# Layer 0's fixed order: where the mean square, the turned-back outputs and the scores for maxima stand

## The chip, the cores and the metric

The kernel runs on one core of one Trainium2 chip. The metric is the device time of one execution in microseconds, the median of the runs shown. A core has five engines that run side by side, each strictly in the order of its own instruction list: TensorE (PE, with its weight loads as PEld), VectorE (DVE), ScalarE (ACT), GpSimd (POOL) and SyncE (SP, which only issues DMAs here). An engine that waits for an operand holds up all that stands behind it in its list.

## The reference

Eight sequences of 256 rows of 512 numbers go through two layers. Each layer adds a gated cross-attention to x and then a gated feed-forward.

```
x = x + tanh(g_xattn[0]) * L0_xattn(layernorm(x), ctx, ctx)   # 16 heads of 32, causal, no weights
x = x + tanh(g_ffn[0])   * L0_ffn(layernorm(x), ...)          # ternary weights, silu(gate)*up,
                                                              # rms_norm over 2048, projection
x = x + tanh(g_xattn[1]) * L1_xattn(layernorm(x), ctx, ...)   # q, k, v, o weights, rms_norm of q and k
x = x + tanh(g_ffn[1])   * L1_ffn(layernorm(x), ...)          # 8-bit activations, ternary weights
```

Layer 0's attention is softmax(q k^T / sqrt(32)) v, with the rows above the diagonal masked; q is the normed x, and k and v are both the context. Its feed-forward is

```
gu = x @ ternary(w_gate_up)^T ; h = silu(gate) * up
out = (h / sqrt(mean(h*h) + eps)) @ ternary(w_proj)^T
```

The mean square is a number for each row, so the kernel multiplies by it behind the projection.

## The kernel before

The 2048 rows are 16 tiles of 128 rows, two for each of the 8 batches. The program has three parts. The first quantizes layer 0's weights, prepares layer 1's keys and values and runs layer 0's attention for batches 0 and 1. The second runs layer 0's feed-forward for batch b (class Feed0), beside layer 0's attention for batch b + 2 (class Attention0), and measures and quantizes layer 1's weights (L922 to L966). The third runs layer 1. The change edits the second part; the attention's `done` of batches 0 and 1 is also used in the first part and at its end.

**How the order is set.** `at(b, (k, step), ...)` gives each step a place: batch b, chunk k, in sixteenths of a batch. `timeline` sorts all steps by place and calls them. In the second part `pe.held` is true, and every PE instruction is tied behind the one called before it, so PE's list is the list of places. The lists of DVE, ACT, POOL and SP are made by a scheduler that follows its own model of the times; the called order is only its priority.

**The feed-forward.** A batch has 16 chunks (8 for each tile of rows). In chunk n PE makes 32 gate/up products into one of two banks "gu" (`hidden`). ACT takes a tanh, DVE multiplies twice (h, L842 and L843; the second one frees the bank), ACT casts the high half (hs, L845), DVE or POOL makes the low half (L295), ACT squares (L848) and POOL adds the square to a sum (acc, L850). Three chunks later PE makes the down product of that chunk into the one bank "y" (`project`). After eight chunks POOL folds the sum (L853), PE adds it over the partitions (`factor`: ssq, into the one bank "o"), DVE and POOL make the power -1/2 of it (rs_t L268, rs_r L270, rgf L887), and DVE adds y, scaled, to x (`add`, L892). `factor` stands before the down product number 7 - AHEAD0 of eight, so with AHEAD0 = 1 before the last but one.

**The attention.** The 16 heads are four groups of four. There are two large score slots (`pair`, PSUM), used in turn by all of the following.

- `ready`: load, layernorm (DVE statistics L277, POOL power L270, POOL y L290), and the turn of y into qT ("turned", PE, then an ACT copy).
- `looks`: four `scores`, each into both slots, DVE takes their maxima (nm, L407, four operations; L415, two, in layer 1's form), then `parts`, ten small POOL operations that split the maxima into three (mz, L427 to L434), then `shift`, where PE turns them (nt) and DVE copies them (nT, L445).
- `weighs`: for each group `exps` (scores the other way round minus the maxima, into both slots, then exp on ACT, p, L481) and `weigh` (products with v and sums into bank "o", copied by ACT, L505, sums added by POOL, L508).
- `done`: PE turns the outputs back ("back", in a score slot) and the sums ("sums", in bank "o"), DVE takes the reciprocal (inv, L569), multiplies (L575) and adds to x (L581).

Behind `done` of batch b + 1 follows Feed0's `ready` of that batch: a layernorm of x, a split into high and low halves (yp, ACT L815 and DVE L816) and a DMA on SP that turns it (xT<-yp).

In the second part the attention of the last batches is followed by `ready` and `looks` of layer 1's attention for batches 0 and 1; its query products ("lin", two halves) take a score slot too, in batches 5 and 6.

The places of the steps before, for the attention that is looked at in batch n:

```
jobs += at(n, *zip((-4.8, -2.4, 4.2 if n == 0 else 0.2), a.ready()))
jobs += at(n, *zip((*((5.4, 7.2) if n == 0 else (1.2, 5.2)), 9.2, 10.4, 10.8, 14.6), a.looks()))
jobs += at(n, *zip((15.3, 18.2, 19.2, 20.2, 22.2, 23.2, 24.2, 25.2), a.weighs()))
jobs += at(n, (27.7, *a.done()))
```

A place over 16 lies in the batch after: 27.7 is chunk 11.7 of batch n + 1.

Of the kernel before, what the change touches and what calls it, by code (L numbers as in the profile page):

```python
# [39 lines left out]
F32 = mybir.dt.float32  # L40
# [5 lines left out]
ALU = mybir.AluOpType  # L46
# [4 lines left out]
P = 128  # L51
B, S, D = 8, 256, 512
NT = B * S // P
NH, HD = 16, 32
DC = D // P
# [22 lines left out]
MP = 3  # L78

LAG = 3  # L80

AHEAD0 = 1

YB = 4

# [4 lines left out]
def flamingo_kernel(  # L90
# [24 lines left out]
    nc = tc.nc  # L115
# [4 lines left out]
    small = ctx.enter_context(tc.tile_pool(name="small", bufs=4))  # L120
    att = ctx.enter_context(tc.tile_pool(name="att", bufs=2))
# [4 lines left out]
    def bank(tag, shape=(P, 512), dtype=F32, name=None):  # L126
        pool, n = part_ps[tag]
        return pool.tile(list(shape), dtype, tag=tag, name=name or tag, bufs=n)

    def banks(stack, name, **tags):  # L130
        pool = stack.enter_context(
            tc.tile_pool(name=name, bufs=1, space=PSUM, reuse_waits="tile")
        )
        part_ps.clear()
        part_ps.update({tag: (pool, n) for tag, n in tags.items()})

    def pair(shape, dtype=F32, name="s"):

        return ps.tile(list(shape), dtype, tag="s", name=name, bufs=2)

    xs = {}
    stage = {}

    def reach(i, n):
        assert stage.get(i, 0) == n - 1, (i, n)
        stage[i] = n
# [4 lines left out]
    def load_x(i, pool):  # L151
        xs[i] = pool.tile([P, D], F32, tag=f"x{i}", name=f"x{i}", bufs=1)
        nc.sync.dma_start(out=xs[i], in_=xf[i * P : (i + 1) * P, :])
# [4 lines left out]
    tg = const.tile([P, 4], F32, name="tg")  # L158
# [4 lines left out]
    ident = const.tile([P, P], F32, name="ident")  # L163
# [97 lines left out]
    pe = Tensor()  # L261
# [96 lines left out]
    class Attention:  # L358
# [3 lines left out]
        n = 0  # L362
# [171 lines left out]
    class Attention0(Attention):  # L534
# [19 lines left out]
            return self.counted(0, [load, norm, turn])  # L554

        def done(self):
            def add():

                t = pair((P, 2, D), name="back")
                sums = bank("o", (P, 2, P), name="sums")  # L560
                for i in range(2):
                    rows = slice(i * P, (i + 1) * P)
                    for c in range(DC):
                        pe.transpose(
                            t[:, i, c * P : (c + 1) * P], self.oT[:, c, rows], ident
                        )
                    pe.transpose(sums[:, i, :], self.sums[:, rows], ident)
                inv = small.tile([P, 2, DC, 4], F32, tag="inv", name="inv", bufs=2)
                nc.vector.reciprocal(  # L569
                    inv, sums.rearrange("p i (r g e) -> p i g r e", r=4, g=DC)[:, :, :, :, 0]  # L570
                )
                for i in range(2):
                    xt = xs[2 * self.b + i]
                    w = self.oT[:, 2 * i : 2 * i + 2, :].rearrange("p c t -> p (c t)")
                    nc.vector.tensor_tensor(  # L575
                        w.rearrange("p (h c) -> p h c", h=NH),
                        t[:, i, :].rearrange("p (h c) -> p h c", h=NH),
                        inv[:, i].rearrange("p g r -> p (g r)").unsqueeze(2).broadcast_to([P, NH, HD]),
                        ALU.mult,
                    )  # L580
                    nc.vector.scalar_tensor_tensor(  # L581
                        xt, w, tg[:, 0:1], xt, ALU.mult, ALU.add
                    )
                    reach(2 * self.b + i, 1)

            return self.finish([add])

    def load_w(pool, name, wT):
        w = pool.tile([P, DC, D], F32, tag=f"w{name}", name=f"w{name}", bufs=1)
# [8 lines left out]
    def timeline(*jobs):  # L598

        steps = []  # L600
        for j, (a, z, job) in enumerate(jobs):
            steps += [(a + (z - a) * (n + 0.5) / len(job), j, step) for n, step in enumerate(job)]
        for _, _, step in sorted(steps, key=lambda e: e[:2]):
            step()

    def at(b, *steps):

        return [(b + n / 16, b + n / 16, [step]) for n, step in steps]
# [150 lines left out]
    att0 = [Attention0(b) for b in range(B)]  # L759
    with ExitStack() as part:  # L760
# [16 lines left out]
        a, z = att0[0], att0[1]  # L777
# [18 lines left out]
    class Feed0:  # L796
# [72 lines left out]
        def step(self, n):  # L869

            if n < HC:
                self.hs[n] = self.hidden(n // 8, n % 8)
            n -= LAG
            if n >= 0:
                if n % 8 == 7 - AHEAD0:
                    self.factor(n // 8)
                self.project(n % 8, self.hs.pop(n))
                if n % 8 == 7:
                    self.add(n // 8)
# [10 lines left out]
        def add(self, i):  # L890
            xt = xs[2 * self.b + i]
            nc.vector.scalar_tensor_tensor(xt, self.ys, self.rg, xt, ALU.mult, ALU.add)  # L892
            reach(2 * self.b + i, 2)
# [35 lines left out]
    def measure1(u):  # L929
        seen[0] += 1  # L930
        w = load1(u)
        a = q1.tile([P, QW], BF, tag="q", name="a1", bufs=2)
        behind(nc.scalar.activation(a, w, AF.Abs, accum_out=l1sum[:, u : u + 1]), block["A"])
# [17 lines left out]
    def quantize1(u):  # L951

        seen[1] += 1
        assert seen[0] == n1
        w = load1(u)
        _, dst, k = units1[u]
        ins = nc.gpsimd.tensor_scalar(w, w, wscale[:, k : k + 1], MAGIC, ALU.mult, ALU.add)  # L957
        behind(ins, block["P"])
        hold1()
        q = q1.tile([P, QW], BF, tag="q", name="q1", bufs=2)  # L960
        nc.gpsimd.tensor_scalar(q, w, 1.0, -MAGIC, ALU.mult, ALU.add)  # L961

        def hold():
            q8 = q1.tile([P, QW], F8, tag="q8", name="q8", bufs=2)
            nc.vector.tensor_scalar(q8, q, 1.0, -1.0, ALU.min, ALU.max, saturate=False)
            nc.sync.dma_start(out=dst, in_=q8.bitcast(U8))  # L966

        left.append(hold)
# [73 lines left out]
    with ExitStack() as part:  # L1042
        banks(part, "ps1", o=1, gu=2, y=1)
        q1 = part.enter_context(tc.tile_pool(name="q1", bufs=1, side="right", reuse_waits="tile"))
        feed0 = [Feed0(b) for b in range(B)]

        def rows(b):
            load_x(2 * b, x2)
            load_x(2 * b + 1, x2)

        jobs = [
            (0.5, 3.0, [lambda u=u: measure1(u) for u in range(n1)]),
            (3.05, 3.05, [scales1]),
            (3.1, 6.5, [lambda u=u: quantize1(u) for u in range(n1)]),
            (6.6, 6.6, [hold1]),
        ]

        jobs += at(0, *zip((-5.0, -4.0), feed0[0].ready()), (-4.5, *att0[1].done()))
        for b in range(B):
            jobs += at(b, *((k, step) for k, step in enumerate(feed0[b].chunks())))
            if b == 0:
                jobs += at(b, *zip((4.4, 5.4), feed0[1].ready()))
            elif b + 1 < B:
                jobs += at(b, *zip((12.4, 13.4), feed0[b + 1].ready()))
        for n, a in enumerate([*att0[2:], *att1[:2]]):
            if n < B - 2:
                jobs += at(n, (-11.0, lambda n=n: rows(n + 2)))  # L1070
                jobs += at(n, *zip((-4.8, -2.4, 4.2 if n == 0 else 0.2), a.ready()))
            else:
                jobs += at(n, *zip((-9.6, -7.6, -4.8, -3.7, -2.6, -2.5, 0.2), a.ready()))
            jobs += at(n, *zip((*((5.4, 7.2) if n == 0 else (1.2, 5.2)), 9.2, 10.4, 10.8, 14.6), a.looks()))
            if a is not att1[1]:
                jobs += at(n, *zip((15.3, 18.2, 19.2, 20.2, 22.2, 23.2, 24.2, 25.2), a.weighs()))
            if n < B - 2:
                jobs += at(n, (27.7, *a.done()))
        pe.held = True
        timeline(*jobs)  # L1080
    w0ctx.close()
# [196 lines left out]
    jobs = []  # L1278
    for b in range(B):
        first, second, a = feed1[2 * b], feed1[2 * b + 1], att1[b]  # L1280
# [76 lines left out]
```

## Time and profile before

| what | value |
|---|---|
| median of 3 runs | 1248.93 us (1246.83 to 1250.46) |
| the profiled execution's own time | 1244.33 us |
| its span, first to last instruction | 1242.6 us |
| mean granted TensorE clock | 0.97 |
| PE, DVE, ACT, POOL busy | 1113.8, 823.0, 611.2, 550.0 us |
| second part (232.5 to 776.0) | 543.5 us |

The profile is one execution. "Granted clock" is the share of full speed that TensorE was allowed. In a row of the timeline the first two numbers are the start and the length in us, then engine, line, operation, output<-inputs, sizes and count; the square brackets give idle time of the engine before it and what ended that. Rows of equal neighbours are merged. In a row of waits the numbers are the total in us, how often, and the longest.

### The profile page before, as it was taken

The numbers are of one execution on the slowest core, as the hardware profiler recorded it, in microseconds if no ns is written. First come the engines' busy times: TensorE is split into PE (matmuls) and PEld (weight loads), VectorE is DVE, ScalarE is ACT, GpSimd is POOL, SyncE is SP. The second block draws the span as 40 slices with busy tenths as digits, with TensorE's granted clock in tenths as the row PEclk, the third lists the DMA queues.
The fourth block names the chain that finished last, engine by engine and source line by source line (L and its number), as shares of the span: only waits on it lengthen the run. The fifth ranks groups of instructions, "written<-read, shape, count | busy, mean of one in ns | idle before, by whom it ended". The sixth has DMA issues, their size and how long they took to land.

```text
span 1242.6 us, 29878 instructions
## 1 busy us (share of the span) xinstructions
PE 1113.8 (90%) x12466; PEld 725.7 (58%) x12565; DVE 823.0 (66%) x1776; ACT 611.2 (49%) x1108; POOL 550.0 (44%) x821
## 2 busy tenths in 40 slices
PE   7988977799999897888999998899999999999976
PEld 3444433577777666666666775455555555555553
DVE  5677797764656455375654645777777777768684
ACT  3446547356575533433344453356464645464663
POOL 3333224353343556465564424826263535424250
PEclk9998888899999998999999999999999999999998
DMA  8343424622333233223222002311212121211231
GB/s 320 127 137 114 158 85 119 221 61 96 120 99 118 64 99 82 82 70 95 84 76 66 19 18 71 109 52 31 64 35 60 35 61 35 61 35 31 39 51 43
DMA packets 101767, 103.91 MB, mean 84 GB/s; under 512 B 61312, under 2 KB 72576, under 8 KB 101632
## 3 DMA queue, kind: packets, MB, share of 16 engines
q1 hardware_dynamic: 98608, 97.01, 26.6%
q10 hardware_dynamic: 3024, 4.98, 1.3%
q8 instruction: 98, 1.61, 0.5%
q14 instruction: 37, 0.30, 0.1%
HBM read 72.09 MB, written 15.73 MB: 71 GB/s over the span
## 4 chain that ended last, share of the span: by engine, by line
PE 29%; DVE 27%; POOL 12%; ACT 8%; issue 5%; DMA 1%; POOLq 0%; DVEq 0%; ACTq 0%
PE gu L256 10%; PE o L256 5%; PE s L256 5%; DVE nm L415 4%; PE y L256 3%; PE py L256 2%; DVE u L1193 2%; DVE h L843 2%; POOL acc L850 2%; DVE ln_st L277 2%; POOL w L957 2%; DVE t L1191 2%; DVE h L842 2%; POOL q L961 2%; DVE umax L1194 2%
## 5 line engine op out<-in xcount | busy, mean ns | idle before, releaser
L256 PE MATMUL gu<-xT,gu 128*128 128x128 f16 x4096 | 254.9, 221 | 11.7 <-DVE h L843 8.3
L256 PEld LDWEIGHTS <-gu 128*128 128x128 bf16 x4096 | 237.7, 99 | 42.2 <-issue 18.6
L850 POOL TENSOR_TENSOR acc<-acc,h 128x256 f32<-128x256 f32 x112 | 83.5, 745 | 130.6 <-ACT h L848 127.0
L256 PE MATMUL gu<-gv,zT 128*128 128x256 fp8e4 x1024 | 131.4, 274 | 10.9 <-ACT gv L1186 6.4
L1186 ACT COPY gv<-gu 128x512 f32<-128x512 f32 x128 | 74.0, 585 | 116.2 <-PE gu L256 108.3
L256 PEld LDWEIGHTS <-zT 128*128 128x128 bf16 x1024 | 96.0, 98 | 57.4 <-issue 36.7
L845 ACT CAST hs<-h 128x256 f16<-128x256 f32 x128 | 51.7, 404 | 147.0 <-DVE h L843 146.6
L842 DVE SCALAR_TENSOR_TENSOR h<-h,gu 128x256 f32<-128x256 f32 x128 | 53.3, 416 | 102.3 <-ACT h L841 97.0
L256 PE MATMUL y<-pr,hs 128*128 128x512 bf16 x413 | 113.5, 383 | 6.9 <-issue 1.4
L270 POOL TENSOR_TENSOR rs_r<-rs_t,mhalf 128x1 f32<-128x1 f32 (+1 forms) x88 | 60.7, 694 | 129.0 <-DVE rs_t L268 108.1
L481 ACT ACTIVATE p<-s 128x768 f32<-128x768 f32 (+1 forms) x128 | 109.8, 908 | 15.1 <-PE s L256 15.1
L415 DVE TENSOR_REDUCE nm<-s 128x4 f32<-128x1024 f32 x64 | 75.8, 1217 | 33.9 <-PE s L256 33.9
L848 ACT ACTIVATE h<-h,hid 128x256 f32<-128x256 f32 x112 | 56.6, 507 | 70.1 <-POOL hs L295 46.6
L508 POOL TENSOR_TENSOR oT<-oT 128x256 f32<-128x256 f32 x48 | 35.3, 735 | 124.3 <-ACT oT L505 124.1
L256 PE MATMUL s<-qT,kT 32*128 32x256 f32 (+1 forms) x1024 | 78.2, 377 | 2.5 <-DVE rs_t L268 1.1
L295 POOL TENSOR_TENSOR hs<-h,hs 128x256 f16<-128x256 f32 x64 | 44.5, 695 | 77.8 <-ACT hs L845 77.8
L841 ACT ACTIVATE h<-gu 128x256 f32<-128x256 f32 x128 | 48.5, 379 | 56.9 <-PE gu L256 56.7
L1191 DVE SCALAR_TENSOR_TENSOR t<-t,gv 128x512 f32<-128x512 f32 x64 | 46.4, 725 | 41.6 <-ACT t L1190 41.6
L256 PE MATMUL s<-kT,qT 32*128 32x256 f32 (+1 forms) x1024 | 68.9, 378 | 2.0 <-DVE nm L415 1.3
L407 DVE TENSOR_REDUCE nm<-s 128x2 f32<-128x256 f32 (+1 forms) x128 | 62.9, 551 | 11.6 <-PE s L256 11.3
L256 PE MATMUL o<-p,v 128*32 128x256 f32 (+1 forms) x1024 | 64.2, 370 | 5.8 <-DVE x L1223 5.6
L256 PEld LDWEIGHTS <-hs 128*128 128x128 f16 x512 | 45.6, 101 | 35.4 <-issue 4.7
(185 smaller groups left out, 2195.4 us busy)
## 6 DMA issues: line engine op xcount, KB each, us to landing
w<-in_gvT_dram SPq DMA_DIRECT2D x32, 512.0 KB, 3.8
w<-in_guT_dram SPq DMA_DIRECT2D x32, 256.0 KB, 3.0
w<-in_outT_dram SPq DMA_DIRECT2D x16, 512.0 KB, 3.6
cT<-in_cxT_dram SPq DMA_DIRECT2D x8, 512.0 KB, 4.9
x<-in_x_dram SPq DMA_DIRECT2D x16, 256.0 KB, 6.6
kT<-in_cxT_dram SPq DMA_DIRECT2D x8, 512.0 KB, 4.0
v<-in_cx_dram SPq DMA_DIRECT2D x8, 512.0 KB, 3.8
vd<-v SPq DMA_DIRECT2D x8, 512.0 KB, 5.3
```

The costliest lines, as they stand in the source:

```text
L256: return self.kept(nc.tensor.matmul(*args, **kwargs))
L270: nc.gpsimd.tensor_tensor(r[:, :n], t[:, :n], mhalf[:, :n], ALU.pow)
L407: nc.vector.tensor_reduce(nm[:, :, qb], s[j][:, :, at[qb] : at[qb] + to[qb]], AX.X, ALU.max, negate=True,)
L415: nc.vector.tensor_reduce(nm, s[j].rearrange("p r (q k) -> p r q k", q=2), AX.X, ALU.max, negate=True)
L481: exp[0] = nc.scalar.activation(self.p[j], s[j][:, :, 0:n], AF.Exp)
L841: block["A"] = nc.scalar.activation(h, gu[:, 0], AF.Tanh, scale=0.5 / UP0)
L842: nc.vector.scalar_tensor_tensor(h, h, 1.0, gu[:, 0], ALU.add, ALU.mult)
L845: nc.scalar.copy(hs[:, 0], h)
L848: nc.scalar.activation(sq, h, AF.Square, scale=hid[:, 1:2])
L850: block["P"] = nc.gpsimd.tensor_tensor(self.acc[i], self.acc[i], sq, ALU.add)
L1186: nc.scalar.copy(self.gv[:, :, k % 2, :], gu)
L1191: nc.vector.scalar_tensor_tensor(t, t, 1.0, g, ALU.add, ALU.mult)
```

## The change

Four things move in the second part, and one tile changes.

1. `factor` stands before the last of the eight down products (n % 8 == 7), one chunk later. AHEAD0 is gone.
2. `done` is two steps, one for each tile of rows, at chunk 26.6 and 27.6 instead of one at 27.7. The first turns its half back, then both halves of the sums, and takes the reciprocal; each multiplies and adds its own half. The product goes to a tile of the tag "y" (four buffers, shared with the layernorms' y) instead of into oT.
3. Feed0's `ready` stands at 11.7 and 12.7 instead of 12.4 and 13.4.
4. The turn of y moves from 0.2 to 1.2, the four `scores` from 1.2, 5.2, 9.2, 10.4 to 3.3, 6.2, 9.3, 12.4, `parts` from 10.8 to 12.6; `shift` stays at 14.6. In `weighs` the second `weigh` moves from 22.2 to 21.2. In layer 1's form the two query products move from -3.7 and -2.6 to -3.3 and -2.4, and what follows them from -2.5 to -2.3.

```diff
         def done(self):
-            def add():
-                t = pair((P, 2, D), name="back")
+            st = {}
+            def divide():
                 sums = bank("o", (P, 2, P), name="sums")
                 for i in range(2):
-                    rows = slice(i * P, (i + 1) * P)
-                    for c in range(DC):
-                        pe.transpose(
-                            t[:, i, c * P : (c + 1) * P], self.oT[:, c, rows], ident
-                        )
-                    pe.transpose(sums[:, i, :], self.sums[:, rows], ident)
-                inv = small.tile([P, 2, DC, 4], F32, tag="inv", name="inv", bufs=2)
+                    pe.transpose(sums[:, i, :], self.sums[:, i * P : (i + 1) * P], ident)
+                st["inv"] = small.tile([P, 2, DC, 4], F32, tag="inv", name="inv", bufs=2)
                 nc.vector.reciprocal(
...
-                for i in range(2):
-                    xt = xs[2 * self.b + i]
-                    w = self.oT[:, 2 * i : 2 * i + 2, :].rearrange("p c t -> p (c t)")
...
+            def add(i):
+                if i == 0:
+                    st["t"] = pair((P, 2, D), name="back")
+                t = st["t"]
+                for c in range(DC):
+                    pe.transpose(
+                        t[:, i, c * P : (c + 1) * P], self.oT[:, c, i * P : (i + 1) * P], ident
+                    )
+                if i == 0:
+                    divide()
+                inv = st["inv"]
+                xt = xs[2 * self.b + i]
+                w = att.tile([P, D], F32, tag="y", name="w", bufs=YB)
...
-            return self.finish([add])
+            return self.finish([lambda: add(0), lambda: add(1)])
...
-                if n % 8 == 7 - AHEAD0:
+                if n % 8 == 7:
                     self.factor(n // 8)
...
-        jobs += at(0, *zip((-5.0, -4.0), feed0[0].ready()), (-4.5, *att0[1].done()))
+        jobs += at(0, *zip((-5.0, -4.0), feed0[0].ready()), *zip((-4.5, -4.4), att0[1].done()))
...
-                jobs += at(b, *zip((12.4, 13.4), feed0[b + 1].ready()))
+                jobs += at(b, *zip((11.7, 12.7), feed0[b + 1].ready()))
...
-                jobs += at(n, *zip((-4.8, -2.4, 4.2 if n == 0 else 0.2), a.ready()))
+                jobs += at(n, *zip((-4.8, -2.4, 4.2 if n == 0 else 1.2), a.ready()))
             else:
-                jobs += at(n, *zip((-9.6, -7.6, -4.8, -3.7, -2.6, -2.5, 0.2), a.ready()))
-            jobs += at(n, *zip((*((5.4, 7.2) if n == 0 else (1.2, 5.2)), 9.2, 10.4, 10.8, 14.6), a.looks()))
+                jobs += at(n, *zip((-9.6, -7.6, -4.8, -3.3, -2.4, -2.3, 1.2), a.ready()))
+            jobs += at(n, *zip((*((5.4, 7.2) if n == 0 else (3.3, 6.2)), 9.3, 12.4, 12.6, 14.6), a.looks()))
             if a is not att1[1]:
-                jobs += at(n, *zip((15.3, 18.2, 19.2, 20.2, 22.2, 23.2, 24.2, 25.2), a.weighs()))
+                jobs += at(n, *zip((15.3, 18.2, 19.2, 20.2, 21.2, 23.2, 24.2, 25.2), a.weighs()))
             if n < B - 2:
-                jobs += at(n, (27.7, *a.done()))
+                jobs += at(n, *zip((26.6, 27.6), a.done()))
```

## The prediction

> **What bounds the kernel now.** I first split the span by the three parts of the program with the busy time by stretch (length; then PE, PEld, DVE, ACT and POOL busy; granted clock; DMA share; GB/s). The change edits only the middle part.
>
> ```profile
> 0.00:232.50 232.50, 191.90 (x1243) 94.69 (x1244) 171.68 (x423) 117.98 (x214) 81.39 (x121) 0.91 0.46 152
> 232.50:776.00 543.50, 497.47 (x7581) 376.30 (x7678) 304.70 (x673) 253.02 (x548) 263.60 (x406) 0.98 0.28 84
> 776.00:1242.60 466.60, 424.46 (x3644) 254.67 (x3644) 346.61 (x680) 240.17 (x346) 204.99 (x295) 0.99 0.20 50
> ```
>
> In the middle part PE is busy for 497.5 of 543.5 us and no other engine for more than 305. PE's order there is written out by hand, so a wait of PE for one operand lengthens the part by that wait. All that can be won is 46 us of PE idle time plus what a lower clock costs. The waits of PE in that part (total us, times, longest):
>
> ```profile
> PE ssq L256 <- POOL acc L853: 10.4, 5, 3.6
> PE gu L256 <- DVE h L843: 8.3, 7, 1.6
> PE ssq L256 <- ACT oT L505: 5.5, 4, 2.3
> PE s L256 <- ACT p L481: 4.3, 7, 0.7
> PE gu L256 <- DMA xT<-yp: 3.3, 3, 1.6
> PE turned L259 <- ACT p L481: 2.0, 1, 2.0
> PE turned L259 <- POOL acc L850: 1.8, 1, 1.8
> PE back L259 <- DVE nm L407: 1.7, 3, 1.1
> PE s L256 <- DVE nm L415: 1.3, 2, 0.8
> ```
>
> The waits cluster in two batches, and there the granted clock falls too (same columns as the first view):
>
> ```profile
> 421.40:496.00 74.60, 63.68 (x1006) 48.55 (x1016) 39.01 (x90) 28.77 (x63) 43.36 (x60) 0.95 0.31 85
> 496.00:571.00 75.00, 63.75 (x1005) 48.08 (x1016) 45.99 (x96) 28.81 (x63) 44.49 (x63) 0.95 0.28 84
> ```
>
> A clock of 0.95 over 75 us is about 3.75 us of lost PE time in each.
>
> **What the change takes away.** Each step is read from the new order, PE's first.
>
> The mean square goes one chunk later (a chunk's gate/up and down products start 2.65 us after one another: 395.59 to 398.24 in the timeline). Its waits, 10.4 for the sum on POOL and 5.5 for bank "o", are at most 3.6 each. The extra chunk, often with a weigh or a turn in it, covers them, except the last one (2.85 us, at 773.8), where no gate/up product is left in between. Gain 13.0.
>
> The turn of y goes one chunk later as well: gain 2.0 + 1.8 = 3.8. The scores of the second group now stand two chunks behind the exponentials, not one: gain 4.3, and 1.3 for the fourth group's. The wait of "back" for the maxima (1.7) goes, because those scores no longer stand just before it. Doing the division for each half of the batch breaks up the block of vector work that held h back: gain 8.3 less 2.0 in the first batch, which keeps its order, 6.3. The layernorm that feeds the transposed x starts 0.7 chunk earlier on paper: gain 3.3. Together 33.7, and with the two dips of the clock (7.5) **41.2 us**.
>
> **What it adds: a late turn of the maxima.** Formerly the fourth group's scores ended at 391.84, the split maxima were ready at 396.1 and turned (nt) at 405.10: cover 13.3 us. Now these scores stand in chunk 12 and nt still in chunk 14, two chunks later: cover 5.3 us. What must run in it shows in these rows, DVE's first, then POOL's:
>
> ```profile
> 392.38 1.95 DVE L407 TENSOR_REDUCE nm<-s 128x2 f32<-128x256 f32 x4
> 395.79 0.36 DVE L569 RECIPROCAL inv<-sums 128x32 f32<-128x32 f32 x1 [0.60 <-PE sums L259]
> 396.19 1.29 DVE L575 TENSOR_TENSOR oT<-back,inv 128x512 f32<-128x512 f32 x2
> 397.39 1.89 DVE L581 SCALAR_TENSOR_TENSOR x<-oT,tg,x 128x512 f32<-128x512 f32 x2
> 399.54 2.46 DVE L277 BATCH_NORM_STATS2 ln_st<-x 128x6 f32<-128x512 f32 x4
> 403.20 0.83 POOL L270 TENSOR_TENSOR rs_r<-rs_t,mhalf 128x2 f32<-128x2 f32 x1 [5.13 <-DVE rs_t L268]
> 404.13 1.52 POOL L290 TENSOR_SCALAR y<-x,ln_mv,rs_r 128x512 f32<-128x512 f32 x2
> 405.62 0.69 POOL L270 TENSOR_TENSOR rs_r<-rs_t,mhalf 128x2 f32<-128x2 f32 x1
> 408.03 1.51 POOL L290 TENSOR_SCALAR y<-x,ln_mv,rs_r 128x512 f32<-128x512 f32 x2
> ```
>
> I count from the end of the third group's scores. PE reaches nt after chunks 10 to 14: five chunks of 2.65, the mean square 0.4, two halves turned back at 0.55 to 0.65, the scores 1.0, about 15.8 us. DVE has in front of the last maxima, in its new order: the third group's maxima 1.95, three h pairs 2.7, the mean square's scaling and its short wait for POOL's power 0.3, the add of y 0.7, two low parts 0.7, the reciprocal 0.4, products 1.2, adds 1.6, statistics 2.4, small ones 0.7, its own 1.95: 14.6 us. So DVE alone leaves 1.2 us for the ten POOL operations of the split, which took 2.2 (393.84 to 396.06). But POOL now has both layernorms in front of them: from the first power, which can start at 12.1, 0.9 + 1.5 + 0.7 + 1.5, one sum (0.72), the split 2.2, a low part (0.67): nt at 20.3, so PE waits about 4.5 us. Laid out entry by entry, with what can overlap, I get 4.1 and 4.4 for batches 1 and 2. In batches 3 and 4 a quantizer step on DVE (0.65) and what waits for POOL's two 1.1 us steps before it come on top: 6.6 and 6.0. In batches 0 and 7 no division stands there: nothing. Sum 21.1. Bounds: the DVE limit alone is 1.0 a batch (4 in all); with every POOL operation stretched as some are (a sum of 0.72 takes 0.95) 28.
>
> In batches 5 and 6 the query product (3.43 us a half) stands right behind these scores and takes the score bank whose maxima come first. It is due at 10.5 and DVE frees that bank at about 13.5: 3.1 us each, 6.2 (bounds 2 to 10). The turn nt is covered there by two query products.
>
> Smaller ones. The sums of the division use bank "o" just after the mean square, whose reading on DVE stands behind a quantizer step that waits for POOL: 0.9 in batches 3 to 5, 2.7 (bounds 0 to 7). Exponentials 2.65 us behind scores of 1.95 us: 0.4 in four batches, 1.6 (0 to 3). The next y product needs the add: 2.2 us after the mean square with 3.6 us until its turn, nothing, but up to 0.8 a batch if POOL's steps come in between. The scheduler also reordered the end of the first part (score slots wait 14 us there) and a few DVE, ACT and SP entries of the third, among them two stores on SP that swap with a transpose: 0, bounds -4 to +4. Moving x's product out of oT frees nothing that is waited for: 0.
>
> **The clock.** Of the waits over 1.9 us in this part, those of 2.75, 3.56 and one of 2.27 were followed by a granted clock of 0.66 over 485 to 495, 0.76 over 563 to 570 and 0.76 over 525 to 532, that is 3.4, 1.7 and 1.7 us lost; another 2.27, a 1.99 and a 2.85 by none. For the four long waits I take 2.6 each, for the two of 3.1 us 1.7 each: 13.8 (bounds 0 to 20).
>
> The Trainium skill (TensorE: Matmul & The Clock Gate, Part 1) says that the array drops to half clock after an idle window of about 3.4 us; the dip after 2.75 us here is shorter than that. By that rule the two 3.1 us waits would cost no clock, and the added cost would be 3.4 lower.
>
> **Sum.** Added 21.1 + 6.2 + 2.7 + 1.6 + 13.8 = 45.4, taken away 41.2: +4.2 us. The profiled execution took 1244.33 (span 1242.6), 0.4% under the median 1248.93. On it the sum gives 1248.5, on the median 1253; I say **1254**, one more for waits that I could not see.
>
> **Rivals.** *Faster: the new order is covered.* If DVE and POOL run the late chain faster than I lay it out, the six new waits shrink below the point at which they break even: (41.2 - 4.3) / 6 = 6.2 us each, clock included; I have 6.9. At their lower bounds (4 + 2, with 1.4 for the rest and a clock loss of 2) 9.4 is added and 41.2 goes: 1217. Halfway, 1235. For it: the maxima were ready 8 us early before. Against it: DVE's list is 14.6 us of work in 15.8.
>
> *Balanced:* the six waits come out within 0.6 us of the break-even point, and the time does not move: 1249.
>
> *Much slower: POOL's quantizer takes over.* If its steps, for which DVE already waited 57 us in 17 waits in this part, fall into the late chain in four batches instead of two, 2.2 us and one more dip each come on top, and the bounds above are reached: 28 + 10 + 7 + 3 + 20 - 41 = +27, 1276.
>
> *The edit of the mean square does nothing*, since POOL's sum is simply late: then 7.5 of the 41.2 stay, 1261. Against it, the sum was ready at 448.3 where PE waited for the bank until 452.35.
>
> **Chances.** My forecast with its neighbours on the slower side has 0.52 (the quantizer 0.1 and the idle mean square 0.07 of it), balanced 0.18, covered 0.30. A difference of 0.3%, 3.7 us, is about what can be told from none. The range 1236 to 1272 leaves out some 0.12 of the covered case and 0.07 at the top; the likeliest case alone has 1250 to 1268.
>
> **What would show it.** Right: PE "nt" waiting for POOL "mz" by 4 us or more in four batches, "lin" waiting for DVE "nm" in two, half clock after them; "ssq" waiting only near the end; "gu" waiting for h and the transposes under 3 us. Wrong: no wait at nt, or one under 2 us, or the waits of "ssq" still over 8 us.

## The result, and the profile after

The changed kernel takes **1275.98 us** (median, 1275.64 to 1277.01) where the kernel before, run beside it, takes 1247.88 (1245.26 to 1250.46): a ratio of 1.0227, 95% interval 1.0203 to 1.0250. It is slower, as forecast, but by 28 us instead of 5, and 4 us beyond the top of the range. The profiled execution has a span of 1275.3 us against 1242.6.

The three parts of the program in the busy time by stretch, with the columns of the first view of the prediction:

```profile
0.00:243.10 243.10, 193.82 (x1243) 95.33 (x1244) 172.62 (x426) 118.26 (x214) 82.64 (x121) 0.89 0.46 150
243.10:808.50 565.40, 503.33 (x7587) 381.70 (x7677) 303.37 (x672) 254.72 (x548) 262.49 (x405) 0.96 0.26 78
808.50:1275.30 466.80, 424.63 (x3644) 254.98 (x3644) 345.42 (x679) 239.95 (x346) 204.60 (x296) 0.99 0.20 50
```

The cut is made at the first gate/up product and at the last add of y. The first part is 10.5 us longer (243.1 against 232.6), the middle part 22.1 (565.4 against 543.35 from the same two marks), the third the same. The prediction had put the whole change into the middle part.

PE's waits from 230 to 810 us of the changed kernel (total us, times, longest):

```profile
PE nt L257 <- POOL mz L432: 27.5, 4, 8.8
PE s L254 <- DVE nm L405: 4.7, 9, 0.7
PE lin L254 <- DVE rs_t L266: 3.8, 1, 3.8
PE sums L257 <- DVE rs_t L266: 3.7, 3, 1.6
PE gu L254 <- DVE h L846: 3.6, 3, 3.0
PE lin L254 <- DVE nm L413: 3.0, 1, 3.0
PE s L254 <- DVE nm L413: 2.7, 4, 0.9
PE y L254 <- DVE x L895: 2.0, 1, 2.0
PE ssq L254 <- POOL acc L856: 2.0, 1, 2.0
```

Beside the list of before: the sum of squares waits 2.0 us instead of 15.9, once and at the end; h and the transposed x 3.6 (all of it for h) instead of 11.6. In their place stands one line, nt waiting for the split maxima (mz), four times, 5.4, 5.7, 8.8 and 7.7 us in batches 1 to 4. The query product (lin) waits in two batches. The 4.7 and 2.7 us of the scores (s) for nm are waits for a score slot whose maxima DVE hasn't read yet.

The longest of those waits, seen from POOL, in the timeline of the changed kernel (start, us, engine, line, operation, output and inputs). The last of DVE's maxima ended at 492.0; PE had nothing left to do from 491.66:

```profile
490.11 2.22 POOL L268 TENSOR_TENSOR rs_r<-rs_t,mhalf 128x2 f32<-128x2 f32 x2 [0.83 <-DVE rs_t L266]
492.33 1.51 POOL L288 TENSOR_SCALAR y<-x,ln_mv,rs_r 128x512 f32<-128x512 f32 x2
494.51 1.95 POOL L288 TENSOR_SCALAR y<-x,ln_mv,rs_r 128x512 f32<-128x512 f32 x2
496.44 0.61 POOL L425 TENSOR_SCALAR mz<-nm 128x16 bf16<-128x16 f32 x2
499.37 0.81 POOL L853 TENSOR_TENSOR acc<-acc,h 128x256 f32<-128x256 f32 x1 [0.63 <-ACT h L851]
500.16 0.36 POOL L432 TENSOR_SCALAR mz<-nmr 128x16 bf16<-128x16 f32 x2
```

POOL does two powers and four scalings of two layernorms first, with one sum between them, from 490.1 to 496.4. Only then does it begin the split, whose input had been ready for 4.4 us, and it puts a low part and a sum between the split's steps. nt starts at 500.4. The clock follows, in the busy time by stretch around that wait:

```profile
488.00:492.00 4.00, 3.61 (x42) 2.40 (x40) 4.00 (x16) 1.18 (x3) 3.08 (x4) 1.00 0.39 119
492.00:501.00 9.00, 0.59 (x6) 0.53 (x7) 4.16 (x9) 3.04 (x7) 8.36 (x19) 0.67 0.23 54
501.00:505.00 4.00, 3.78 (x33) 3.44 (x33) 1.16 (x3) 0.38 (x1) 2.35 (x3) 0.50 0.47 82
```

POOL is busy for 8.4 of the 9 us in which PE does nearly nothing, and PE then works at 0.50. The records have half clock from 495.1 to 505.3, beginning 3.4 us into the wait and lasting 4.9 us beyond its end: 2.45 us lost on top of the 8.75.

### The profile page after: what moved, and what is told of

Read it like the earlier page. It is cut to its first block, busy times and chain, and to the rows that moved or that the text cites. A ratio compares the mean times of both kernels' runs of the same rounds, so it can differ in the third digit from the quotient of the medians.

```text
span 1275.3 us, 29894 instructions
## 1 busy us (share of the span) xinstructions
PE 1121.8 (88%) x12473; PEld 732.0 (57%) x12565; DVE 821.4 (64%) x1776; ACT 612.9 (48%) x1108; POOL 549.7 (43%) x821
## 4 chain that ended last, share of the span: by engine, by line
PE 30%; DVE 28%; POOL 11%; ACT 8%; issue 5%; DMA 1%; POOLq 0%; DVEq 0%; ACTq 0%
PE gu L254 11%; PE s L254 5%; PE o L254 5%; DVE nm L413 4%; PE y L254 3%; DVE h L846 2%; PE py L254 2%; DVE ln_st L275 2%; DVE u L1196 2%; DVE h L845 2%; POOL rs_r L268 2%; DVE t L1194 2%; POOL w L960 2%; PE proj L254 2%; POOL q L964 2%
## 5 line engine op out<-in xcount | busy, mean ns | idle before, releaser
L254 PE MATMUL gu<-xT,gu 128*128 128x128 f16 x4096 | 259.5, 223 | 3.6 <-DVE h L846 3.6
L254 PEld LDWEIGHTS <-gu 128*128 128x128 bf16 x4096 | 242.8, 100 | 31.7 <-issue 17.0
L254 PE MATMUL gu<-gv,zT 128*128 128x256 fp8e4 x1024 | 130.6, 273 | 10.8 <-ACT gv L1189 6.4
L479 ACT ACTIVATE p<-s 128x768 f32<-128x768 f32 (+1 forms) x128 | 109.7, 907 | 15.1 <-PE s L254 15.1
L254 PE MATMUL lin<-wq,xT 128*128 128x512 f32 x128 | 63.4, 642 | 11.0 <-DVE rs_t L266 3.8
```

The lines of the kernel that those rows point to most:

```text
L254: return self.kept(nc.tensor.matmul(*args, **kwargs))
L479: exp[0] = nc.scalar.activation(self.p[j], s[j][:, :, 0:n], AF.Exp)
```

## The experiments

Each median stands beside runs of the kernel before on the same chip (medians 1246.8 to 1248.8); the number behind it is the ratio to these, with its 95% interval in brackets. Two marks cut the profile: the first gate/up product (end of the first part) and the last add of y (end of the middle part). Before they give 232.65 and 543.35 us for the two parts, after 243.1 and 565.4.

**e1: scores and split back to their old places.** The changed kernel with

```
-  (3.3, 6.2)), 9.3, 12.4, 12.6, 14.6), a.looks()))
+  (3.3, 6.2)), 9.2, 10.4, 10.8, 14.6), a.looks()))
```

> The changed kernel with one thing undone: the fourth group's scores and the split of the maxima stand at 10.4 and 10.8 again (the third group's at 9.2). Theory (the late turn of the maxima is the main cost of the second part): the four waits of nt for mz (27.5 us) and the two of lin (6.8) go, and with them most of the half-clock stretches that follow; some 2 to 4 us come back at the turned-back outputs, which again stand right behind scores. About 1276 - 36 = 1240; the first part stays 10 us longer than in the kernel before. Rival (vector and POOL work is simply late, and the wait moves to whatever comes next, back or gu): 1262 or more, with PE's waits in the second part above 45 us.

1255.73 us, 1.0073 [1.0058, 1.0088]. The waits of nt and of lin for maxima are gone, and the middle part is 545.1 us, 20 less: the late places are what costs there. The rest of the hoped gain is eaten by a line that neither theory had at this size:

```profile
PE back L257 <- DVE nm L405: 14.8, 5, 4.1
```

The first half of the split division now comes right behind the scores at 10.4, and "back" takes a score slot whose maxima DVE hasn't read.

**e2: the mean square alone.** The kernel before with `AHEAD0 = 0` in place of 1.

> The kernel before with only the mean square one chunk later. If the wait is covered by the extra chunk: ssq waits fall from 15.9 to about 3 us, the two dips of the clock go in part, first part unchanged: 1248 - 13 - 4 = 1231 to 1238. Rival (the wait moves to the next user of bank o or to the y product behind the add): 1245 to 1250. A third reading, that the square's move made the changed kernel slow: over 1255.

1244.23 us, 0.9980 [0.9968, 0.9993]. The waits of the sum of squares fall from 15.9 to 2.3, but the time only by 2.5, nearer to the rival than to the theory. The scores now reach slot and exponentials earlier and wait 8.9 us for them instead of 4.3, in ten waits; h and others take more of it in small pieces.

**e3: the division in two halves alone**, with its steps at 26.6 and 27.6 and Feed0's layernorm at 11.7 and 12.7 as changed.

> The kernel before with only the division in two steps (its product in a y tile, the next layernorm at 11.7). If the 10 us that the first part lost come from the split of the division there: first gate/up product about 10 us later; second part gains up to 9 of h and transpose waits, some given back at sums: 1248 + 10 - 6 = 1252 (1247 to 1258). Rival (the first part's loss is not the split's): first part as before, 1240 to 1245.

1273.64 us, 1.0216 [1.0197, 1.0234], 16 us above the band. First gate/up product at 241.1: the split of the division lengthens the first part, as expected. What the expectation lacked stands in the middle part (557.4): "back" waits 15.3 us for nm, as in e1, and the sum of squares still 16.5.

**e4: the places alone.** The kernel before with only the new numbers for ready, looks and weighs.

> The kernel before with only the places of the turn, the scores, the split of the maxima and the second weigh moved. Theory: nt waits in four batches, 20 to 35 us in all, lin waits in two, half clock behind them; the mean square's waits stay in part; the first part unchanged: 1260 to 1275. Rival (the late chain is late only because the division is split): nt waits under 8 us, 1240 to 1248.

1281.51 us, 1.0278 [1.0263, 1.0294], 6 us above the band. The first part stays at 232.4; the middle part takes 575.8, with nt waiting 24.3 us although the division is whole. With e1 this puts the late chain down to the places from both sides, and not to the split of the division.

**e5: the turn of the maxima one chunk later**, 15.1 instead of 14.6.

> The changed kernel with the turn of the maxima (nt) one chunk later, 15.1 instead of 14.6, so 2.65 us more work stands in front of it. Theory (the split of the maxima on POOL comes at a fixed time, PE waits for the rest): the four waits of nt, 5.4 + 5.7 + 8.8 + 7.7 = 27.5 us, fall by 2.65 each to about 17, the exponentials now stand directly behind nt and wait for its copy, +0.8 each; 1276 goes to about 1267. Rival (the wait is only handed on, since the exponentials need the turned maxima anyway and the chunk in between is late too): nt 17 but the exponentials wait over 2 us in each batch, time 1274 to 1278.

Three executions took 1267.1 to 1271.1 us, 1.0162 [1.0114, 1.0210]; the profiled one took 5372 us and is left out, so there is no profile to read. That is some 5 us less than the changed kernel, between the 9 of the theory and the 0 of the rival: some of the cover is won, and it can't be said what takes the rest.

**e6: the first part's division whole.** In the changed kernel, for batch 0 only, `return self.finish([whole])` with the former body.

> The changed kernel with the division of batch 0, the one that stands in the first part, put back to one step with its product in oT; all else as changed. Theory (splitting that one division costs the first part its 10 us): the first gate/up product is back at 232 to 234 us instead of 243, the rest of the span unchanged, 1266. Rival (the first part is longer because of the places of later work): first gate/up product still at 241 to 243 us, 1276.

1267.75 us, 1.0145 [1.0100, 1.0191]; first gate/up product at 234.2 instead of 243.1, the middle part within 1.5 us of the changed kernel's. 8 to 9 us of the miss go with this one division.

**e8, e13 and e14: what it is in that division.** e8 calls both halves in one step. e13 is the kernel before with only the product of that division moved into a y buffer. e14 is the changed kernel with that product outside the y buffers.

> The changed kernel with both halves of batch 0's division called in one step in the first part, one behind the other, the products still in the y buffers. Beside e6 it tells two causes of the 10 us apart. If it is the two steps standing apart in the first part's order: first gate/up product at 232 to 235 us, 1267. If it is the y buffers, which that division now shares with the next batch's layernorm: still at 241 to 243 us, 1276.

> The kernel before with one thing changed: the product of the first part's division (batch 0) goes into the y buffers instead of oT, its transposes and sums as before. If the y buffers, which it then shares with the layernorms, make the first part longer: first gate/up product at 240 to 243 us, 1256. If the order of the split transposes and sums does: 232 to 234 us, 1248.

> The changed kernel with the division of the first part split as changed, but its products outside the y buffers (the first half in a buffer of its own, the second in oT). If the y buffers make the first part longer: first gate/up product at 232 to 235 us, 1267. If the order of the split transposes and sums does: 240 to 243 us, 1276.

e8: 1274.97 us, first gate/up product at 241.2. e13: 1248.36, ratio 1.0000 [0.9989, 1.0012], first product at 232.5. e14: 1273.65, 239.7. So the buffer alone costs nothing (e13), and neither one step (e8) nor other buffers (e14) bring the short first part back; e8's expectation, which left only the buffer, had one cause too few. What the three long ones share is the order of transposes and sums: the second half is turned back only behind the product of the first. PE's order in the first part isn't fixed by hand, so the scheduler lays other work in between. The transposes of batch 0 in the timeline, before and then after:

```profile
145.27 0.82 PE L259 MATMUL back<-ident,oT 128*128 128x128 f32 x6
146.36 0.38 PE L259 MATMUL back<-ident,oT 128*128 128x128 f32 x2
146.98 0.27 PE L257 MATMUL back<-ident,oT 128*128 128x128 f32 x1
155.27 0.60 PE L257 MATMUL back<-ident,oT 128*128 128x128 f32 x4
```

Before, both halves are turned back within 1.5 us (in e6 too). After, the second half comes 8 us behind the last transpose of the first, as in e8 and e14, and its score slot is taken for that long. In these three the scores of the first part wait 8.0 to 8.5 us for a slot whose maxima aren't read, where before and in e6 it was 4.7, and the product "top_b" near its end waits 4.3 to 6.0 us instead of 2.3. In the changed kernel that is 5.6 of the 10.5 us. That the slot held longer is what makes these waits is read from the traces, not tested, and the rest was not traced. The quantizer's means on PE are not what tells the long first parts from the short: between 140 and 172 us there are seven before and in e6 and five after, but in e8 seven as well.

**e7 and e9: the layernorms behind the split.** e7 moves the feed's layernorm from 11.7 to 12.7, behind the split at 12.6. e9 also lays the order on POOL down, in the middle part:

```
-  nc.gpsimd.tensor_tensor(r[:, :n], t[:, :n], mhalf[:, :n], ALU.pow)
+  behind(nc.gpsimd.tensor_tensor(r[:, :n], t[:, :n], mhalf[:, :n], ALU.pow), last)  # last step of the split
```

> The changed kernel with the layernorm that feeds the next batch at 12.7 and its turn at 13.7, instead of 11.7 and 12.7: it then stands behind the split of the maxima (12.6) on POOL, and its statistics behind the last maxima on DVE. Theory (the two layernorms in front of the split make nt late): nt waits fall from 27.5 us in four batches to under 8, with the half clock behind them; the transposed x is later, up to 4 us of waits for it come back; 1276 goes to about 1254. Rival (DVE's maxima alone are late, or POOL's other steps): nt still waits over 18 us, 1270 or more. Second rival (the transposed x becomes the bound): nt near 0 but products wait over 12 us for xT, 1268 or more.

> The changed kernel with the order on POOL laid down in the second part: both layernorms (their powers and scalings) stand behind the split of the last maxima, instead of in front of it (moving the place of the layernorm alone, in the run before, left the order of the instructions as it was). Theory (the layernorms on POOL hold the split): the split takes the 2.2 us that it took before the change, from the end of the maxima at 351.0, 418.9, 492.0 and 567.8 us of the changed kernel's profile, where PE reached nt at 351.8, 419.7, 491.6 and 567.8; nt waits 1.4 + 1.4 + 2.6 + 2.2 = 7.6 us instead of 27.5, and some of the half clock goes too; the transposed x comes later, 0 to 4 us; about 1254. Rival (DVE's maxima, or the sums and low parts on POOL, hold it): nt still waits over 16 us, 1266 or more.

e7 took 1276.02 us with the same 27.5 us at nt: POOL and DVE are ordered by the scheduler, and there the other place changed almost nothing, so the run tells nothing of the theories. e9 took 1264.95, 1.0145 [1.0112, 1.0178]. In its waits of PE:

```profile
PE nt L257 <- POOL mz L434: 7.2, 8, 1.7
PE gu L254 <- DMA xT<-yp: 5.8, 4, 2.7
PE s L254 <- DVE nT L447: 2.0, 2, 1.0
```

nt falls to 7.2 us, where the theory worked out 7.6. The middle part falls by 13, not 20, since 7.8 us are handed on to the transposed x, now later, and to the copy behind nt. The size of the wait was right (by batch 1.2, 1.2, 2.5 and 2.3, for 1.4, 1.4, 2.6 and 2.2), what follows it was put too low, and the first part still takes 241.2.

**e10: the statistics on DVE behind the maxima as well**, `behind(nc.vector.bn_stats(st, t), split["V"])`.

> The same, and on DVE too: the statistics of both layernorms stand behind the last maxima. Theory (what stands in front of the chain of maxima, split and nt makes it late, on both engines): maxima end about 2.4 us earlier, nt waits under 4 us in all, waits of the lin product for maxima shrink; about 1250. Rival (the time is handed on to the transposed x, which now comes later): nt near 0, but products wait 10 us or more for xT, or for the sum of squares, 1262 or more.

1257.10 us, 1.0080 [1.0053, 1.0107]. nt waits 1.9 us, lin 4.5 instead of 6.8; the transposed x waits 7.9. The middle part takes 543.8 us, what it took before the change: taking the late chain of maxima, split and nt away takes back all 22 us that this part had lost, but none of the hoped gain shows. The expected 1250 left the first part out again, here 243.6.

**e12: e10 with the first part's division whole.**

> The changed kernel with the order of e10 on POOL and DVE and the division of the first part whole as in e6: if the two causes add up, 8 us under e10, about 1242, first gate/up product at 233 to 235 us. If the gains are not independent: at the time of e10 or above.

1261.65 us, 1.0115 [1.0089, 1.0141]: 4.5 above e10. The first part only falls to 239.3, where the same whole division gave 234.2 in e6, and the other two grow (548.2 and 470.6). So a whole division doesn't by itself give a short first part, and the gains don't add; the scheduler orders each program afresh, and which of its choices costs these microseconds was not found.

**e11 and e16: what of the change is left when nothing late stands in front of the maxima.** e11 is the kernel before with

```
-AHEAD0 = 1
+AHEAD0 = 0
...
-  (-4.8, -2.4, 4.2 if n == 0 else 0.2), a.ready()))
+  (-4.8, -2.4, 4.2 if n == 0 else 1.2), a.ready()))
...
-  (5.4, 7.2) if n == 0 else (1.2, 5.2)), 9.2, 10.4, 10.8, 14.6), a.looks()))
+  (5.4, 7.2) if n == 0 else (3.3, 6.2)), 9.2, 10.4, 10.8, 14.6), a.looks()))
```

and e16 the same with AHEAD0 left at 1.

> The kernel before with only the parts of the change that put nothing in front of the maxima: the mean square one chunk later, the turn of y one chunk later (1.2), the first two groups' scores at 3.3 and 6.2; the division whole, the third and fourth groups' scores and the split at 9.2, 10.4 and 10.8 as before. Theory: the 9 us of waits of scores for exponentials that the mean square alone had are taken by the later scores, and the 3.8 of the turn go: 1236 to 1241. Rival (the waits move on to the third group's scores, now 3 chunks behind instead of 4, or to back): 1244 to 1250.

> The kernel of e11 without the later mean square: only the turn of y at 1.2 and the first two groups' scores at 3.3 and 6.2. If the mean square's waits (15.9 us before) are won only where the later scores give cover, and both edits are needed: the waits of the sum of squares stay at 12 to 16 us, 1240 to 1246. If the later scores and the turn make the whole gain of e11: 1229 to 1234.

e11 takes **1231.24 us**, 0.9872 [0.9847, 0.9896], the fastest of all kernels here and 5 us under the expected band. e16 takes 1252.06, 1.0036 [1.0023, 1.0048], above both of its bands. The mean square alone won 2.5 us, the later turn and scores alone lose 4, both together win 16.5. The exponentials in e2 and then e11, and the sum of squares in e16 and then e11:

```profile
PE s L256 <- ACT p L481: 8.9, 10, 2.3
PE s L256 <- ACT p L481: 1.3, 3, 0.5
PE ssq L256 <- POOL acc L853: 15.7, 8, 4.4
PE ssq L256 <- POOL acc L853: 3.2, 3, 2.0
```

Each edit alone leaves one of the two waits, and longer than before (8.9 us where it was 4.3; 15.7 and 4.2 more for bank "o" where it was 15.9 in all); only both remove both. And the clock, e11's middle part by stretch:

```profile
232.59:762.00 529.41, 496.68 (x7680) 372.91 (x7678) 308.38 (x676) 252.09 (x548) 263.46 (x405) 1.00 0.29 86
```

A granted clock of 1.00: but for the first 4 us, which a wait in the first part left behind, there is no half clock before the last add, and no wait of PE is over 2.0 us. e2, at 0.98, has PE busy for 504.8 us with as many products: 8 of the 12.6 us between the two middle parts are PE time, which goes with the clock.

**e15: e11 with the second weigh at 21.2 and the last batches' ready steps at their new places.**

> The kernel of e11 (mean square, turn and first two scores later) with the two sets of places of the change that no run has had alone: the second weigh at 21.2, and the last two batches' ready steps at -3.3, -2.4, -2.3 and 1.2. Theory: they put nothing in front of anything waited for, within 2 us of e11, 1229 to 1233. Rival (the query products of the last batches meet the maxima): 1235 or more.

1233.36 us, 0.9891 [0.9875, 0.9906], just over the expected band: these edits are worth nothing, or cost 2 us.

## Why the prediction was right and wrong

**The direction and its cause were right.** The turn nt waits for mz in batches 1 to 4 and not in 0 and 7, lin in two others, the sum of squares only at the end. Only the sign for h, under 3 us, was just missed (3.6). POOL's two layernorms in front of the split are the reason (e9), DVE's list in front of the maxima the rest (e10).

**What failed, by its terms:**
- *"The scheduler also reordered the end of the first part ...: 0, bounds -4 to +4."* It measured +10.5. This is the largest miss: the same edit that was credited with 6.3 us for h in the middle part was costed at nothing where the first part also runs it, and the bounds came from no row. The prediction had seen score slots waited for 14 us there and gave a division that takes its slot for longer no price; these waits are now 17.6 us. e6 gives 8 to 9 of it back, e8, e13 and e14 leave the order of transposes and sums; how that order makes the rest of the part longer stays open, and e12 shows that it is no fixed price.
- *nt, "Sum 21.1", bounds 4 to 28:* 27.5, near the upper bound. In the longest wait the split's own 2.2 us became 4.1 (496.4 to 500.5), since a low part and a sum come in between, and a power in front of it that was put at 0.9 took 1.55. By batch the misses are 1.3, 1.3, 2.1 and 1.7.
- *"Exponentials 2.65 us behind scores ... 1.6 (0 to 3)", with 1.3 won for the maxima of the fourth group:* scores waited 7.4 us for maxima (4.7 and 2.7) where before it was 1.3. The term asked whether the exponentials had time; what was short was the score slot, whose maxima DVE reads later than before.
- *"The next y product needs the add: ... nothing":* 2.0 us once.
- *"Taken away ... 33.7":* without the 1.3 just counted 32.4; by the list it is 30.7 (13.9 for the sum of squares, 3.4 turn, 3.7 exponentials, 1.7 back, 4.7 h, 3.3 transposed x). The sum was near for this program, but e2 and e16 show that it wasn't a sum of parts: the 13.0 of the mean square are worth 2.5 alone.

**Right in size:** lin 6.8 us (6.2), sums 3.7 (2.7), third part 0. The clock: the seven stretches of half clock reach 4.8, 4.9, 4.9 and 4.9 us beyond the ends of the nt waits and 3.3, 6.2 and 3.2 beyond those of two lin and one h, half of 32 us is 16 lost, against 13.8 added by the forecast; the dips of before, counted the same way, had cost 6.6, not 7.5.

The misses are 10.5 + 6.4 + 5.8 + 2.0 + 1.7 in the order of this list, 3.1 for the clock and 1.6 for lin and sums, together 31.1 us, where the span was missed by 28.5 (32.7 against 4.2); the difference of 2.6 us wasn't traced. The rival "much slower" had the right time (1276) by luck: the quantizer took part in two batches only, as in the forecast, and a third of its price is the first part.

**The rule on the clock.** The prediction went by the length of a single wait, and had found waits of 2.27 us with and without a dip. In each trace all stretches of half clock begin on one grid with steps of 3.41 us (in these middle parts they last one to three steps), and what tells these waits apart is how much of one step PE is idle. Here are the steps with the two waits of 2.27 us in the kernel before (length, PE busy, granted clock, DMA share, GB/s):

```profile
448.33:451.75 3.42, 1.75 (x32) 1.00 0.39 110
523.43:526.84 3.41, 1.21 (x22) 1.00 0.53 165
```

The first wait (450.08 to 452.35) reaches into the next step; PE was idle for 0.49 of this one, and the clock stayed full. The second (524.64 to 526.91) lies almost wholly in one step, 0.64 of it idle, and the next step was granted 0.50. Counted over all 17 traces, the 188 steps at full clock in which PE was idle for 0.6 or more were all followed by half clock, and none of the 5004 in which it was idle for less than 0.3; of the 513 in between, 63 were. So a wait of about 2 us can cost a step at half clock, and so can two shorter ones: in e2 waits of 1.79 and 0.50 us in one step (up to 435.49) did.

The Trainium skill (TensorE: Matmul & The Clock Gate, Part 1) states a free-running window of about 3.4 us and half clock after an idle one. The grid of 3.41 us agrees with it. Read as "no wait under 3.4 us costs clock", as the prediction put it, it doesn't hold here: a window that was idle for 0.6 was enough every time.

## What to carry to other kernels

Before a step is moved later in a fixed order, list what stands in front of its whole chain on each engine that it runs through; here nt needed 2.2 us of POOL work and in its longest wait got it behind 6.3 us of layernorms and a sum. An edit in a shared function is to be costed at every place that calls it, above all where the order is left to a scheduler. And waits on one in-order engine are not won one by one: take two edits that give each other cover together (e11) before either is judged alone.

## What the runs showed of the hardware that was not expected

Short steps on POOL are stretched beside some DVE steps and not beside others. The power of 128x2 took 1.55 us at 490.11, beside the quantizer's step (q) and a low part (hs) on DVE, and 1.21 at 419.25, beside the low half of y (yp). Right behind the first, at 491.63, it took 0.69 with DVE just as busy, with maxima (nm) and h.

The clock is decided step by step of 3.41 us, so small waits count by how they fall. The middle parts of e2 and e11, with longest waits of 2.3 and 2.0 us, had granted clocks of 0.98 and 1.00 and differ by 8 us of PE time.
